# Slot numbers carried in the node's row, one-hot columns made ahead, and the adjacency matrix loaded in two parts

## The chip, the cores and the metric

One core of a Trainium2 chip runs the whole kernel. The time is the device time in microseconds (us) of one execution. The names of the engines are those of the profile: PE is TensorE (PEld its weight loads), DVE is VectorE, ACT is ScalarE, POOL is GpSimd, SP is SyncE. P = 128 is the number of partitions, N = 2048 the nodes, so there are NT = 16 tiles of 128 nodes, and 16 tiles of 128 rows of the adjacency matrix (1 MB each).

## The reference, cut to what matters

Four graph layers follow one another, each with a residual and a layer norm. Only the first one is touched. Its work on 8 graphs with 2048 nodes, 64 features and 64 hyperedges is:

```python
h = x @ W                                             # per node
alpha = softmax(where(H.T > 0, leaky_relu(h @ a_node), NEG))   # per hyperedge, over nodes
agg = einsum('ben,bnf->bef', alpha, h)                # 64 hyperedges: a small table
beta = sigmoid((h @ a_gn)[:, None, :] + (agg @ a_ge)[:, :, None])
all_he = elu(beta * h + (1 - beta) * agg)             # per pair (hyperedge, node)
se = tanh(elu(agg) @ fcW + fcb) @ av
coefs1 = softmax(where(H > 0, se, NEG))               # per node, over its hyperedges
g = einsum('bne,benf->bnf', coefs1, all_he)           # the loop that the change is about
deg = maximum(adj.sum(-1), 1.0)
industry = einsum('nm,bmf->bnf', adj / deg, x @ W_ind)  # the large product, beside it
# ... attention over (industry, g), residual, layer norm; then layers 1 to 3
```

Few pairs (hyperedge, node) are set in H. The kernel sorts the nodes by how many hyperedges they have (`order`), and handles a tile of 128 sorted nodes slot by slot: slot s is the s-th hyperedge of each node. A one-hot matrix (hyperedge by node) picks the right row of the table with a matrix product.

## The kernel before

First phase: for each tile of nodes a projection `ph`, exponentials, a sum over nodes `pagg` for the table, and a row of 520 values (features and gates) written to HBM. The adjacency streams in meanwhile and is cast.

```python
def load_adj(t):
    for k in range(2):
        a = pa.tile([P, HN], F32, tag="a", name="a", bufs=4)
        nc.sync.dma_start(a, adj_t[t * P:(t + 1) * P, cols(k, HN)])
        if t < NT - XT:  nc.gpsimd.tensor_copy(adj[t][:, cols(k, HN)], a)     # tiles 0 to 11
        else:            nc.scalar.copy(adj[t][:, cols(k, HN)], a)            # tiles 12 to 15
# ... cut ...
hs = pa.tile([P, NT, E], F32, name="hs")         # the mask's rows in sorted order
for t in range(NT):
    nc.gpsimd.indirect_dma_start(out=hs[:, t, :], in_=h_ne, in_offset=... order[:, t:t + 1] ...)
# ... cut ...
for t in range(NT):                              # the first phase's loop
    # 4 products into ph, exponentials, products with them (DVE), then:
    nc.scalar.dma_start(hs_hbm[t * P:(t + 1) * P, :], st)      # row: 512 features, 8 gates
    for k in range(2):
        nc.tensor.matmul(pagg[:, k, ...], lhsT=m_n[:, t, :], rhs=ex[:, k] ...)
xs_scope.close()                                 # frees the room of adjacency tiles 12 to 15
for t in range(NT - XT, NT): load_adj(t)
degrees(0, 8)                                    # 4 products per tile: column sums of adj
# slot numbers: compares, 16 transposes, 4 products with a triangle of ones, into `slot`
# table of the hyperedges and se, with degrees(8, 10), (10, 12), (12, 16) between; ts2
```

The row gathers follow, and a loop over 16 tiles of sorted nodes. PE is filled up in it with the products `u` of the industry term, x split into a high and a low half (`v0h`, `v0l`, ...) against the resident adjacency.

```python
def split(pool, src, tag, bufs, shape):
    nc.scalar.copy(hi, src)
    nc.vector.tensor_tensor(lo, src, hi, ALU.subtract)         # low half on DVE

def begin(t):
    hrow = pl.tile([P, BF + 8], F32, tag="hrow", name="hrow", bufs=2)
    nc.gpsimd.indirect_dma_start(out=hrow, in_=hs_hbm[:], in_offset=... order[:, t:t + 1] ...)
    both = split(pb, hrow[:, 0:BF], "hr", 2, [P, BF])
    for s in range(S):                                         # S slots in this tile
        nc.gpsimd.tensor_scalar(o, slot[:, cols(t, P)], float(s + 1), None, op0=ALU.is_equal)
        mm(ps[:, s] ..., lhsT=o, rhs=ts2)
    # R, rs, co: small operations of DVE

now = begin(0)
for t in range(NT):
    for s in range(S):
        mm(pz, ...)                          # 3 products: row high, row low, table by one-hot
        if s == 0 and t + 1 < NT:
            fill(3); now = begin(t + 1)
        fill(8)                              # 8 products u
        nc.vector.tensor_tensor(z, z, R ...)           # DVE, in PSUM
        nc.scalar.activation(y, z, AF.Exp, bias=-1.0)  # ACT
        nc.vector.scalar_tensor_tensor(y, z, 1.0, y, op0=ALU.max, op1=ALU.min)
        # s == 0: acc = y * co on DVE; else y = y * co on DVE, acc += y on POOL
```

Of the kernel before, what the change touches and what calls it, by code (L numbers as in the profile page):

```python
# [56 lines left out]
def tile_gnn_fast(  # L57
# [6 lines left out]
    h_ne: bass.AP,  # L64
# [24 lines left out]
    E = h_ne.shape[1]  # L89
# [72 lines left out]
    def split(pool, src, tag, bufs, shape):  # L162

        hi = pool.tile(shape, F32R, tag=f"{tag}h", name=f"{tag}h", bufs=bufs)
        lo = pool.tile(shape, F32R, tag=f"{tag}l", name=f"{tag}l", bufs=bufs)
        nc.scalar.copy(hi, src)  # L166
        nc.vector.tensor_tensor(lo, src, hi, ALU.subtract)
        return hi, lo
# [33 lines left out]
    slot = hy.tile([P, N], BF16, name="slot")  # L202

    inv_row = hy.tile([P, N], F32, name="inv_row")
    tri2 = hy.tile([P, P], BF16, name="tri2")
    nc.vector.memset(tri2, 0.0)
    make_upper_triangular(nc, tri2[0:E, 0:E], 1.0, diag=True)
    nc.vector.tensor_copy(tri2[E:P, E:P], tri2[0:E, 0:E])

    hs_hbm = dram.tile([N, BF + 8], F32, name="hs_hbm")  # L210
# [7 lines left out]
    XT = NT // 4  # L218
    adj = [adj_pool.tile([P, N], F32R, name=f"adj{t}") for t in range(NT - XT)]




    with tc.tile_pool(name="pa", bufs=1) as pa, tc.tile_pool(name="pa_ps", bufs=1, space=PSUM) as pps:
# [3 lines left out]
        nc.sync.dma_start(m_n, h_ne.rearrange("(t p) e -> p t e", p=P))  # L228
# [15 lines left out]
        def load_adj(t):  # L244

            HN = N // 2
            for k in range(2):
                a = pa.tile([P, HN], F32, tag="a", name="a", bufs=4)
                nc.sync.dma_start(a, adj_t[t * P:(t + 1) * P, cols(k, HN)])
                if t < NT - XT:  # L250
                    nc.gpsimd.tensor_copy(adj[t][:, cols(k, HN)], a)
                else:
                    nc.scalar.copy(adj[t][:, cols(k, HN)], a)

        for t in range(NT - XT):
            load_adj(t)
# [59 lines left out]

        tl = pa.tile([P, NT], F32, name="tl")
# [29 lines left out]

        hs = pa.tile([P, NT, E], F32, name="hs")
        for t in range(NT):
            nc.gpsimd.indirect_dma_start(  # L350
                out=hs[:, t, :], out_offset=None, in_=h_ne,
                in_offset=bass.IndirectOffsetOnAxis(ap=order[:, t:t + 1], axis=0),
            )

# [19 lines left out]
        for t in range(NT):  # L374
            ph = pps.tile([P, 2, C], F32, tag="ph", name="ph", bufs=2)
            for p in range(NP):
                nc.tensor.matmul(
                    ph[:, p // 2, (p % 2) * 2 * (F + 2):(p % 2 + 1) * 2 * (F + 2)], lhsT=xt[t][:, p, :],
                    rhs=bd66.rearrange("p b f -> p (b f)"), start=True, stop=True,
                )  # L380
            hv = ph[:, :, 0:G * (F + 2)].rearrange("p k (g c) -> p k g c", c=F + 2)
            st = pa.tile([P, BF + 8], F32, tag="st", name="st", bufs=2)
            ex = pa.tile([P, 2, G, F + 1], F32, tag="ex", name="ex", bufs=2)
            sv = seen[:, t].rearrange("p (k g) c -> p k g c", k=2)
            nc.vector.tensor_scalar(
                sv, hv[:, :, :, F:F + 2], CLIP, -CLIP, op0=ALU.min, op1=ALU.max
            )
            e_gn = st[:, BF:BF + 8]
            nc.scalar.activation(e_gn.rearrange("p (k g) -> p k g", k=2), sv[:, :, :, 1], AF.Exp)
            lr = pa.tile([P, B], F32, tag="lr", name="lr", bufs=2)  # L390
            nc.vector.scalar_tensor_tensor(
                lr, seen[:, t, :, 0], 0.2, seen[:, t, :, 0], op0=ALU.mult, op1=ALU.max
            )
            nc.scalar.activation(ex[:, :, :, F], lr.rearrange("p (k g) -> p k g", k=2), AF.Exp)
            for k in range(2):
                nc.vector.scalar_tensor_tensor(
                    st[:, k * G * F:(k + 1) * G * F].rearrange("p (g f) -> p g f", f=F), hv[:, k, :, 0:F], 1.0,
                    e_gn[:, k * G:(k + 1) * G, None].to_broadcast([P, G, F]), op0=ALU.add, op1=ALU.mult,
                )
            nc.vector.tensor_tensor(  # L400
                ex[:, :, :, 0:F], hv[:, :, :, 0:F], ex[:, :, :, F:F + 1].to_broadcast([P, 2, G, F]), ALU.mult
            )
            nc.scalar.dma_start(hs_hbm[t * P:(t + 1) * P, :], st)
            for k in range(2):
                nc.tensor.matmul(
                    pagg[:, k, 0:G * (F + 1)], lhsT=m_n[:, t, :], rhs=ex[:, k].rearrange("p g c -> p (g c)"),
                    start=t == 0, stop=t == NT - 1,
                )
# [6 lines left out]
        for t in range(NT - XT, NT):  # L415
            adj.append(adj_end.tile([P, N], F32R, name=f"adj{t}"))
            load_adj(t)


        du = [pps.tile([P, 2, C], F32, tag="ph", name=f"du{g}", bufs=2) for g in range(2)]  # L420
        ones_r = pa.tile([P, P], F32R, name="ones_r")
        nc.gpsimd.tensor_copy(ones_r, ones)

        def degrees(first, end):
            for t in range(first, end):
                for c in range(NCH):
                    mm(
                        du[c // 2][:, c % 2, :], lhsT=ones_r, rhs=adj[t][:, cols(c)],
                        start=t == 0, stop=t == NT - 1,
                    )  # L430

        degrees(0, 8)


        for c in range(NCH):
            m2 = pa.tile([P, JT, 2, E], F32, tag="m2", name="m2", bufs=2)
            for i in range(2):
                nc.vector.tensor_scalar(m2[:, :, i, :], hs[:, c * JT:(c + 1) * JT, :], 0.0, None, op0=ALU.is_gt)
            pt = pps.tile([P, C], F32, tag="sm", name="pt", bufs=2)
            for j in range(JT):  # L440
                nc.tensor.transpose(pt[:, cols(j, P)], m2[:, j].rearrange("p i e -> p (i e)"), ident)
            mt = pa.tile([P, C], BF16, tag="mt", name="mt", bufs=2)
            nc.scalar.copy(mt, pt)
            pcm = pps.tile([P, C], F32, tag="sm", name="pcm", bufs=2)
            nc.tensor.matmul(pcm, lhsT=tri2, rhs=mt, start=True, stop=True)
            nc.vector.tensor_tensor(slot[:, cols(c)], pcm, mt, ALU.mult)
# [12 lines left out]
        tab = pa.tile([E, B, F], F32, tag="st", name="tab", bufs=2)  # L459
# [21 lines left out]
        degrees(8, 10)  # L481
# [7 lines left out]
        degrees(10, NT - XT)  # L489
# [4 lines left out]
        degrees(NT - XT, NT)  # L494
# [9 lines left out]
        for g in range(2):  # L504
            nc.scalar.copy(inv_row[:, cols(g, 2 * C)], du[g].rearrange("p k c -> p (k c)"))
# [34 lines left out]
    with ExitStack() as pb_scope:  # L540
        pb = pb_scope.enter_context(tc.tile_pool(name="pb", bufs=1, side="right"))
        pps = pb_scope.enter_context(tc.tile_pool(name="pb_ps", bufs=1, space=PSUM))
        def products():
# [3 lines left out]
            def fetch(p, c):  # L547
                xc[p, c] = pb.tile([P, JT, P], F32, tag="x", name="xc", bufs=4)
                load_x(xc[p, c], p, c)
# [3 lines left out]
            def parts(p, c):  # L553
                part[c] = split(pb, xc.pop((p, c)), f"v{c}", 1, [P, JT, P])

            for c in range(NCH):
                fetch(0, c)
            for c in range(NCH):
                parts(0, c)
            deg1 = pb.tile([P, NT], F32, name="deg1")  # L560
            for p in range(NP):
                for g in range(2):
                    own = (2 * g, 2 * g + 1)
                    u = {c: pps.tile([P, C], F32, tag=f"u{c}", name=f"u{c}", bufs=1) for c in own}
# [36 lines left out]

        filler = products()
# [6 lines left out]

        def begin(t):  # L610

            hrow = pl.tile([P, BF + 8], F32, tag="hrow", name="hrow", bufs=2)
            nc.gpsimd.indirect_dma_start(
                out=hrow, out_offset=None, in_=hs_hbm[:],
                in_offset=bass.IndirectOffsetOnAxis(ap=order[:, t:t + 1], axis=0),
            )
            S = sum(n > t for n in SLOT_TILES)
            both = split(pb, hrow[:, 0:BF], "hr", 2, [P, BF])
            ohs = []
            ps = pps.tile([P, 12, 2, B], F32, tag="ps", name="ps", bufs=1)  # L620
            for s in range(S):
                o = pl.tile([P, P], F32R, tag="o", name="o", bufs=17)
                nc.gpsimd.tensor_scalar(o, slot[:, cols(t, P)], float(s + 1), None, op0=ALU.is_equal)
                ohs.append(o)
# [15 lines left out]

        now = begin(0)
        for t in range(NT):
            S, both, ohs, R, co = now
            acc = pl.tile([P, B, F], F32, tag="acc", name="acc", bufs=2)
            for s in range(S):
# [6 lines left out]
                fill(8)  # L652
# [15 lines left out]

    hy_scope.close()
# [459 lines left out]
def tile_gnn_general(  # L1129
# [643 lines left out]
    "x", "x_t", "adj_t", "h_ne", "w0", "w_ind", "a_node", "a_gn", "a_ge", "fc_w", "fc_b", "av", "w1_t",  # L1773
    "emb", "emb_t", "w_pool", "b_pool", "iv", "w31_t", "b31", "w32_t", "w32", "b32", "w0_t",
# [66 lines left out]
```

## Time and profile before

| | before |
|---|---|
| median of 4 runs beside the changed kernel | 2229.9 us (2225.27 to 2233.65) |
| last product of the first phase (`pagg` ends) | 78.9 us |
| G: first row gather | 101.3 us |
| first product with a low half of x | 114.2 us |
| end of the loop (last product u) | 293.1 us |
| from there to the end | 1934.1 us |

### The profile page before, as it was taken

The page shows a single profiled execution, that of the slowest core. Times are in us where ns is not written, and L with a number is a line of the kernel's source. Part 1 is how long each engine was busy: PE and PEld are TensorE (multiplying, and loading weights), DVE is VectorE, ACT ScalarE, POOL GpSimd, SP SyncE. Part 2 cuts the span into 40 slices and gives each one's busy share as a digit, 9 for nine tenths or more (in the row PEclk, how much of TensorE's full clock was granted, in tenths as well). Part 3 has the DMA queues.
Part 4 walks back from the last instruction along what each step waited for, and adds up shares of the span by engine and source line. Part 5 has one row for each costly group of instructions (what it writes and reads, how often), then busy time and mean ns, then how long its engine had stood idle before and what let it go on. Part 6 is the DMA issues. An engine that isn't in the chain of part 4 may idle for free.

```text
span 2227.2 us, 19810 instructions
## 1 busy us (share of the span) xinstructions
PE 1993.1 (89%) x7318; PEld 1289.3 (58%) x7318; DVE 1139.1 (51%) x1900; ACT 338.3 (15%) x584; POOL 551.0 (25%) x499
## 2 busy tenths in 40 slices
PE   7799978888759999799999999999986989999994
PEld 4488745555644444375456456447434777777873
DVE  5479956666532222216864773782784344331312
ACT  1322323222111111010010001001000011111110
POOL 5457466564323323200110110110010001010202
PEclk7889989999969999999999999999998999999997
DMA  8723334322210000000000000000001223200000
GB/s 263 237 66 91 95 91 107 83 70 63 76 46 0 19 19 19 19 24 5 10 5 3 10 8 1 10 8 3 8 8 32 76 72 85 62 19 1 20 1 21
DMA packets 99306, 103.26 MB, mean 46 GB/s; under 512 B 63088, under 2 KB 63136, under 8 KB 99008
## 3 DMA queue, kind: packets, MB, share of 16 engines
q1 hardware_dynamic: 73248, 83.09, 12.8%
q0 software_dynamic: 4064, 9.10, 1.7%
q10 hardware_dynamic: 21888, 9.70, 1.6%
q8 instruction: 60, 0.98, 0.2%
q14 instruction: 46, 0.38, 0.1%
HBM read 75.59 MB, written 26.28 MB: 46 GB/s over the span
## 4 chain that ended last, share of the span: by engine, by line
PE 63%; DVE 12%; DMA 12%; POOL 7%; issue 4%; ACT 2%; SPq 0%; ACTq 0%; POOLq 0%; DVEq 0%
PE py L967 18%; PE u L171 17%; PE u L914 10%; PE u L527 9%; DMA fcav<-in_adj_t 7%; POOL ln_r L155 3%; PE pz L171 2%; DVE fcav L1061 2%; PE pf L171 1%; PE pr L171 1%; DMA x<-x_hbm 1%; DVE ln_v L151 1%; DVE ln_c L145 1%; DVE ln_m L143 1%; ACT r L149 1%
## 5 line engine op out<-in xcount | busy, mean ns | idle before, releaser
L967 PE MATMUL py<-wp,xg 128*128 128x512 f32 x1024 | 448.5, 597 | 8.5 <-DVE fcav L972 5.8
L967 PEld LDWEIGHTS py<-wp,xg 128*128 128x128 f32 x1024 | 193.6, 191 | 254.4 <-issue 216.4
L171 PE MATMUL u<-adj,hi 128*128 128x512 f32 x768 | 256.5, 415 | 0.0
L171 PE MATMUL u<-adj,lo 128*128 128x512 f32 x768 | 246.5, 400 | 1.1 <-DVE lo L1026 1.1
L914 PE MATMUL u<-pt,xn 128*128 128x512 f32 x512 | 227.5, 603 | 8.3 <-DVE u L923 7.1
L972 DVE TENSOR_TENSOR fcav<-py,emb_n 128x512 f32<-128x512 f32 x256 | 177.0, 691 | 52.0 <-PE py L967 37.5
L975 POOL TENSOR_TENSOR r<-r,bias 128x256 f32<-128x256 f32 x32 | 23.3, 729 | 636.0 <-DVE r L973 636.0
L973 DVE TENSOR_REDUCE r<-fcav 128x32 f32<-128x512 f32 x256 | 175.4, 685 | 8.1
L914 PEld LDWEIGHTS u<-pt,xn 128*128 128x128 f32 x512 | 97.3, 193 | 130.2 <-issue 114.7
L527 PE MATMUL u<-adj,vh 128*128 128x512 f32 x512 | 158.3, 408 | 15.4 <-ACT vh L166 11.6
L171 PEld LDWEIGHTS u<-adj,hi 128*128 128x128 f32 x768 | 143.2, 190 | 40.8 <-issue 11.5
L171 PEld LDWEIGHTS u<-adj,lo 128*128 128x128 f32 x768 | 144.6, 190 | 35.4 <-DVE lo L1026 1.6
L527 PE MATMUL u<-adj,vl 128*128 128x512 f32 x512 | 152.1, 398 | 0.0
L155 POOL TENSOR_TENSOR ln_r<-ln_e,neg_half 128x8 f32<-128x8 f32 x64 | 106.1, 1658 | 174.9 <-DVE ln_e L153 166.9
L908 DVE TENSOR_SCALAR pt<-pt 128x512 f32<-128x512 f32 x64 | 49.1, 784 | 172.8 <-ACT pt L907 171.3
L1045 POOL TENSOR_TENSOR r<-r,xn 128x512 f32<-128x512 f32 x16 | 20.4, 1275 | 418.9 <-DVE r L1044 418.9
L527 PEld LDWEIGHTS u<-adj,vh 128*128 128x128 f32 x512 | 96.2, 189 | 45.7 <-ACT vh L166 13.1
L912 POOL TENSOR_TENSOR acc<-acc,pt 128x512 f32<-128x512 f32 x60 | 79.6, 1327 | 162.6 <-DVE pt L908 159.8
L527 PEld LDWEIGHTS u<-adj,vl 128*128 128x128 f32 x512 | 96.4, 189 | 22.1 <-issue 0.7
L1061 DVE SCALAR_TENSOR_TENSOR fcav<-fcav,adj 128x512 f32<-128x512 f32 x64 | 44.5, 695 | 117.6 <-DMA fcav<-in_adj_t 117.1
L149 ACT ACTIVATE r<-ln_c 128x512 f32<-128x512 f32 x64 | 40.4, 631 | 288.4 <-DVE ln_c L145 274.8
L709 POOL DMA_INDIRECT gn<-gs_hbm,rank x64 | 69.7, 1088 | 34.7 <-issue 14.2
(316 smaller groups left out, 2774.3 us busy)
## 6 DMA issues: line engine op xcount, KB each, us to landing
a<-in_adj_t SPq DMA_DIRECT2D x32, 512.0 KB, 5.9
fcav<-in_adj_t SPq DMA_DIRECT2D x64, 256.0 KB, 2.8
x_hbm<-r SPq DMA_DIRECT2D x20, 256.0 KB, 2.3
hs_hbm<-st ACTq DMA_DIRECT2D x16, 260.0 KB, 5.4
xt<-in_x_t SPq DMA_DIRECT2D x16, 256.0 KB, 5.4
u_hbm<-ut SPq DMA_DIRECT2D x16, 256.0 KB, 2.7
gs_hbm<-acc SPq DMA_DIRECT2D x16, 256.0 KB, 2.0
ut<-u_hbm SPq DMA_DIRECT2D x16, 256.0 KB, 3.2
```

Source lines behind the costliest of these rows:

```text
L149: nc.scalar.activation(r, xc, AF.Square)
L155: nc.gpsimd.tensor_tensor(rstd, vare, neg_half[:, :groups], ALU.pow)
L171: tc.keep_in_program_order(nc.tensor.matmul(*args, **kw))
L527: nc.tensor.matmul(u[c], lhsT=half[:, j, :], rhs=adj[t][:, cols(c)], start=t == 0 and i == 0, stop=ends and not own,)
L709: nc.gpsimd.indirect_dma_start(out=gn[:, j, :], out_offset=None, in_=g_rows, in_offset=bass.IndirectOffsetOnAxis(ap=rank4[:, p, c * JT + j ...
L908: nc.vector.tensor_scalar(pt, pt, 1.0, None, op0=ALU.max)
L912: nc.gpsimd.tensor_tensor(acc, acc, pt, ALU.add)
L914: nc.tensor.matmul(u[p], lhsT=xn[p][:, t, :], rhs=pt, start=t == 0, stop=t == NT - 1)
L967: nc.tensor.matmul(py.rearrange("p o d -> p (o d)"), lhsT=xg[b][:, q, cols(j, P)], rhs=wp[:, q, cols(k)], start=q == 0, stop=q == 1,)
L972: nc.vector.tensor_tensor(pr, py, e_b, ALU.mult)
L973: nc.vector.tensor_reduce(r[:, j, b, cols(k, OH)], pr, AX.X, ALU.add)
L1061: nc.vector.scalar_tensor_tensor(a, a, 1.0, adj[t][:, cols(k)].bitcast(F32), op0=ALU.mult, op1=ALU.not_equal, accum_out=left[:, t, k:k + 1],)
```

## The change

Its intent, as far as it can be read from the code: take the slot numbers out of POOL's sixteen mask gathers (they are computed at the front in node order and travel in the row that is gathered anyway), prepare the one-hot columns before their tile begins, and let the first row gather start without waiting for the whole adjacency. Nine tiles are loaded before it and seven after. The degrees, which need all tiles, become the first filler products of the loop. Side changes come with it, above all four: row buffers 2 to 4, load buffers 4 to 3, the low halves of x on POOL, and all casts of the adjacency on POOL.

```diff
-    def split(pool, src, tag, bufs, shape):
+    def split(pool, src, tag, bufs, shape, eng=nc.vector):
-        nc.vector.tensor_tensor(lo, src, hi, ALU.subtract)
+        eng.tensor_tensor(lo, src, hi.bitcast(F32) if eng is nc.gpsimd else hi, ALU.subtract)
+    HROW = BF + 8 + E
+    EARLY = 9
-                a = pa.tile([P, HN], F32, tag="a", name="a", bufs=4)
+                a = pa.tile([P, HN], F32, tag="a", name="a", bufs=3)
-        for t in range(NT - XT):
+        for t in range(EARLY):
             load_adj(t)
+        mt = pa.tile([E, N], BF16, name="mt")
+        nc.vector.tensor_scalar(mt, m_en, 0.0, None, op0=ALU.is_gt)
+        for t in range(NT):
+            nc.tensor.matmul(pcm[:, t, :], lhsT=mt[:, cols(t, P)], rhs=tri_e, start=True, stop=True)
+        nc.vector.tensor_tensor(slot, pcm, m_n, ALU.mult)
-        hs = pa.tile([P, NT, E], F32, name="hs")            # and 16 gathers of the mask
-            st = pa.tile([P, BF + 8], F32, tag="st", name="st", bufs=2)
+            st = pa.tile([P, HROW], F32, tag="st", name="st", bufs=4)
+            nc.scalar.copy(st[:, BF + 8:], slot[:, t, :])
-        for t in range(NT - XT, NT):
-            load_adj(t)
-        degrees(0, 8)                                       # and the old slot numbers
+        some_degrees(5)                                     # later 2 and 2; 28 products stay
@@ the loop @@
-                part[c] = split(pb, xc.pop((p, c)), f"v{c}", 1, [P, JT, P])
+                part[c] = split(pb, xc.pop((p, c)), f"v{c}", 1, [P, JT, P], nc.gpsimd)
+            yield from degree_passes
+        def load_adj_end(t):
+            for c in range(NCH):
+                a = pb.tile([P, JT, P], F32, tag="x", name="a", bufs=XB)...   # shared with x
+                nc.sync.dma_start(a, adj_t[t * P:(t + 1) * P, cols(c)])
+                tc.keep_in_program_order(nc.gpsimd.tensor_copy(adj[t][:, cols(c)], a))
+        def slots(t):
+            transpose(pt, hrows[t][:, BF + 8:])
+            for i in range(2):
+                nc.scalar.copy(slot[i * E:(i + 1) * E, :], pt)
+            # then one is_equal per slot on POOL, kept in one_hot[t]
+        fetch_rows(0)
+        fetch_rows(1)
+        for t in range(EARLY, EARLY + 2):
+            load_adj_end(t)
+        slots(0)
+        for t in range(EARLY + 2, NT):
+            load_adj_end(t)
         now = begin(0)
+        slots(1)
-                fill(8)
+                fill(4 if t == 0 and s < 6 else 8)
+                if s == max(0, S - 5) and t + 2 < NT:
+                    slots(t + 2)
```

## The prediction

> **What bounds the kernel now.** I read first the page's table of 40 slices and its chain by line. TensorE (PE) is busy 89% of 2227 us, and all the lines that cost much (L967, L914, L527, the products with the adjacency after 293 us) belong to later layers. The order in which each engine issues after the loop over 16 tiles of nodes is the same in both builds (ACT, POOL and SP word for word), so I carry that part, 293 us to the end, over unchanged. All that can move lies in 0 to 293 us. There I took the busy time by stage:
>
> ```profile
> core 0: us, PE busy (x) PEld busy (x) DVE busy (x) ACT busy (x) POOL busy (x), PEclk, DMA share, GB/s
> 16.00:60.00 44.00, 35.19 (x157) 22.59 (x157) 26.18 (x80) 4.42 (x20) 27.05 (x27) 0.73 0.82 265
> 60.00:79.00 19.00, 14.22 (x56) 8.25 (x57) 14.08 (x33) 3.24 (x12) 11.35 (x12) 0.73 0.92 321
> 79.00:101.00 22.00, 19.00 (x88) 13.29 (x87) 6.04 (x14) 12.16 (x18) 2.22 (x2) 1.00 0.65 207
> 101.00:113.00 12.00, 6.62 (x16) 4.82 (x17) 2.45 (x8) 2.89 (x5) 10.58 (x18) 0.50 0.55 133
> 113.00:135.00 22.00, 21.47 (x82) 17.46 (x81) 10.60 (x24) 2.83 (x5) 9.11 (x10) 0.66 0.33 72
> 135.00:239.00 104.00, 104.00 (x477) 85.72 (x476) 99.32 (x180) 34.37 (x59) 74.56 (x74) 1.00 0.28 82
> 239.00:264.00 25.00, 21.45 (x95) 16.84 (x93) 24.96 (x47) 7.47 (x13) 10.27 (x9) 1.00 0.26 85
> ```
>
> The reader sees three regimes: DMA near its limit until 79 us, a seam from 79 to 113 us in which nothing is full except POOL at the end, and then a loop in which PE is full, with VectorE (DVE) hardly less so, and DVE alone full at 239 to 264 us. The chain that ended last names what holds the first two:
>
> ```profile
> 52.26 5.42 DMA hs<-in_h_ne,order
> ...
> 64.77 7.27 DMA hs_hbm<-st
> ...
> 94.40 4.22 DMA a<-in_adj_t
> 98.62 0.02 issue
> 98.65 1.04 ACT adj L253
> 99.69 0.92 ACT inv_row L505
> 100.61 0.70 issue
> 101.31 6.49 DMA hrow<-hs_hbm,order
> ```
>
> The first gather of rows (hrow, 101.31) waits for the last adjacency tile, its cast on ACT and the evacuated degrees. Before that, the gathers of the mask (hs) stand in POOL's queue and hold both DVE and the loads. The waits of 0 to 101 us, those of the load queue and of ACT, say it again:
>
> ```profile
> SPq L249 <- POOL adj L251: 39.6, 21, 7.8
> ACT st L389 <- DVE seen L385: 38.0, 11, 9.4
> ACT st L389 <- DMA hs_hbm<-st: 16.7, 5, 6.0
> ```
>
> **What the Trainium skill says.** "DMA: Bandwidth & Descriptors", Specifications, puts HBM for one core at about 358 GB/s. The trace agrees roughly: stretches of 4 us in which the DMA is over 92% busy show 282 to 389 GB/s, a little over the page at the top. "TensorE: Matmul & The Clock Gate", Part 1, says that PE runs at half clock after an idle window and needs some 3.4 us of work to come back. The trace agrees: granted clock 0.50 at 101 to 113 us, where PE waits for one-hots, and 0.66 in the next stage. "GPSIMD Engine Reference", 3.1, says that a two-input elementwise operation is nearly twice as slow on GpSimd as on VectorE. The trace agrees: acc (128x512) takes 1294 ns on POOL in the middle, a like product on DVE 680 ns. "SBUF — State Buffer", Who interferes with whom, says that such operations of both engines lock each other out. The loop's acc mean of 1381 ns over that median fits, though it doesn't prove it.
>
> **The change, part by part.**
>
> (1) Slot numbers move to the front. Gone are 16 mask gathers on POOL (15.4 us busy, 23 us with their waits), 8 DVE compares, 16 PE transposes and 4 products. New at about 11 to 14 us are a DVE compare of 64x2048 (twice the 0.76 us of the 128x1024 one, 1.5 us), 16 small bf16 products (some 1.3 us) and one DVE product of 128x1024 (1.2 us). In the build these stand ahead of the first ph products, so the first pagg goes from 16.3 to about 20 us: 3 to 4 us lost. Gained is the pause at 40 to 44 and 57 to 62 us, where PE waited 2.95 us and 4.72 us for DVE behind the mask gathers.
>
> (2) Row writes with four buffers. A tile costs PE 1.06 us for ph and 1.06 us for pagg: 2.15 us at full clock, as at 32 to 40 us. But in ACT's order of the changed build the slot copy for tile k+2 stands before the second exp of tile k and waits for the write of tile k-2. So four buffers help little more than two, and with a write landing in 5.4 us (median) the beat is about (5.4+0.8)/2 = 3.1 us while loads fill the DMA. Adjacency loads before the seam shrink from 16.8 to 9.4 MB, so they end at some 52 us; the beat falls to 2.15 us from there. Tiles 0 to 3 done at 35.5 us, then 12 tiles at 2.4 us on the mean: pagg ends near 64.5 us instead of 78.9.
>
> (3) The seam. From pagg's end to ts2 it is 14.7 us now (78.9 to 93.6). With 20 instead of 32 degree products ahead of pht it becomes about 12.5 us. The gather then waits for nothing of the later adjacency: it goes at G = 64.5 + 12.5 = 77 us instead of 101.3. That is 24 us gained at this point.
>
> (4) The price: tile 0. Seven adjacency tiles (7.3 MB, 22 us at 330 GB/s) now load after G, 28 casts of 128x512 on POOL. In POOL's order of the changed build, between the first gather and the first low half v0l, stand: 4 gathers x 1.15 = 4.6 us; 17 one-hots x 0.555 = 9.4; 28 casts x 0.57 (between half of the 1.05 us cast of 1024 and the 609 ns least copy of 512) = 16.0; 5 acc x 1.29 = 6.5; v0l 1.3. Sum 37.8 us, and some 3 us until the first row and slots are there: 41 us. PE reaches the first product with v0l (pz of 8 slots and 28 degree products done) only then, at 77 + 41 = 118 us. Before, it had this at 114 us. So part 4 eats all of the 24 us and more; only the work done in the meantime remains as gain.
>
> (5) The rest of the loop, PE's bill from the chain: 8 products u take 1.83 us (0.229 each), a pz triple 0.70, ps 0.115. After v0l: 512 x 0.229 = 117.2; 49 pz x 0.70 = 34.3; 40 ps x 0.115 = 4.6; pdc about 3 (now 4.57 at half clock); pinv 1.8; 14 new slot transposes x 0.11 = 1.5. Sum 162.4 us. The loop now: 117.2 + 56 x 0.70 + 45 x 0.115 + 4.57 + 1.8 = 168 us of 180 us from 112.8 to 292.9, so 12 us are lost to half clock at the start and to DVE at 239 to 264 us. The 16 low halves v (x 0.68 = 11 us) leave DVE for POOL, which has room (POOL was 72% busy at 135 to 239 us). I put the loss at 7 us: 169.4 us. End of loop 118 + 169 = 287 us against 293: about 6 us gained.
>
> **The rivals.** (A) POOL blocks less than I count, or the ph loop runs at PE's beat throughout: G near 72, tile 0 in 37 us; end at 278 us, time 2214. For it: the parameters look tuned. Against: the order in POOL's queue. (B) The first phase stays bound by DMA. 19.5 MB have to pass before G (x 4.2, adjacency 9.4, rows 4.8, masks 1.0); at the 265 GB/s of 16 to 60 us that is 73 us, and pagg ends at 70 us or later, the writes still on the path: loop end at 293 us or more, time 2230. For it: three load buffers instead of four. Against: the 265 GB/s was measured with POOL holding the loads. (C) POOL becomes the bound in the steady loop: low halves waiting for PE and ACT hold acc, y has two buffers, DVE and PE stop behind it. 16 halves with 1 us each would make 2238. For it: POOL executes in order. Against: a quarter of its time was free. (D) All 24 us are kept, if tile 0 hides behind PE's own work: 2203. Against: PE has only some 13 us of work there.
>
> **Range and chances.** My sum gives 2229.6 - 6 = 2223 us. Each us of G and of tile 0 counts fully; I am unsure by 5 us on each, by 4 on the loop's losses, so about 8 us in all: 2207 to 2236. Two per cent is 44.6 us; the whole seam and tile 0 are worth less, so faster by over 2% has a chance of 0.02, slower by over 2% 0.01, the rest 0.97.
>
> **What would show it.** Right: the first row gather at 72 to 82 us; pagg ending 12 to 13 us before; from there 38 to 45 us in which POOL is over 85% busy, PE not; the first v0l product near 118 us, waiting for POOL; DVE busy less by some 10 us in the loop, and the stage before its end with less PE idle time; the end of the loop near 287 us; the time from there to the end within 2 us of before. Wrong: a first gather after 85 us (the ph loop is still held by the row writes), PE at work through tile 0 (POOL cheaper than counted), or new waits of PE for the low halves or of ACT for acc in the steady loop.

## More of the kernel before

From the page of the kernel before, busy time and share of the span by engine:

```profile
span 2227.2 us, 19810 instructions
PE 1993.1 (89%) x7318; PEld 1289.3 (58%) x7318; DVE 1139.1 (51%) x1900; ACT 338.3 (15%) x584; POOL 551.0 (25%) x499
```

The shares are averages over four layers. Only the first 293 us can change, and there they differ from stage to stage. So the milestones above are what to compare; each is the start or end of one instruction in the timeline. A sum over them tells where a difference was made: first phase up to G, the first tile (G to the first low-half product), the loop proper, the rest.

## The result, and the profile after

The changed kernel took 2247.38 us in the median of 4 runs (2244.34 to 2249.93) against 2229.9 us. The ratio is 1.0079 with a 95% interval of 1.0054 to 1.0104. Its output is correct. Ratios here and below are the mean time of one kernel's fast runs over the mean of the other's in the same rounds, so not quite the ratio of the medians quoted.

Within 2% it is "the same", yet it is slower by more than the runs scatter, and lies outside the predicted range. Set against the milestones of before:

| us | before | predicted | after |
|---|---|---|---|
| `pagg` ends | 78.9 | 64.5 | 73.7 |
| G: first row gather | 101.3 | 77 | 86.6 |
| first product with a low half | 114.2 | 118 | 135.8 |
| end of the loop | 293.1 | 287 | 311.7 |
| from there to the end | 1934.1 | 1934 | 1936.4 |

The loss is made in the loop's stretch alone. Loop end: -14.7 us up to G, +36.3 us in the first tile (12.9 before, 49.2 now), -3.0 us in what follows (178.9 before, 175.9 now). That makes +18.6 us; the rest adds 2.3 us, which is within what it varies between runs of one instruction order (1925 to 1941 us over the runs below).

Busy time by stage of the changed kernel, with columns as in the prediction's first fence:

```profile
core 0: us, PE busy (x) PEld busy (x) DVE busy (x) ACT busy (x) POOL busy (x), PEclk, DMA share, GB/s
16.00:60.00 44.00, 32.05 (x163) 20.96 (x162) 27.65 (x92) 6.59 (x35) 16.64 (x16) 0.84 0.88 299
60.00:74.00 14.00, 11.94 (x66) 7.80 (x66) 9.64 (x30) 2.38 (x13) 2.08 (x2) 1.00 0.49 172
74.00:86.60 12.60, 10.76 (x60) 8.35 (x58) 5.18 (x13) 3.16 (x8) 0.03 (x1) 0.96 0.00 1
86.60:110.00 23.40, 10.86 (x29) 8.02 (x30) 5.81 (x16) 2.77 (x7) 17.25 (x29) 0.50 0.52 162
110.00:135.00 25.00, 17.11 (x42) 10.35 (x41) 11.49 (x17) 5.65 (x9) 20.24 (x27) 0.70 0.79 223
135.00:190.00 55.00, 53.85 (x248) 43.51 (x248) 36.80 (x62) 17.30 (x34) 36.87 (x35) 0.92 0.26 70
```

Two things are to be seen. From 74 to 86.6 us the DMA engines stand still (1 GB/s): the late loads take over memory of the first phase and wait for its last operation (their queue waits 11.4 us for the table `ts`). And in the 48 us after G, the stage of the first tile, no engine is full: PE works 28 us at clocks of 0.50 and 0.70, POOL 37.5 us, and the DMA, now carrying 7.3 MB that used to arrive earlier, is busy half to four fifths of the time. Before, this stretch had 12.9 us.

The waits of the changed kernel, engine and line, what was waited for, us in total, times, and the longest; from 0 to 87 us:

```profile
POOL hrow L621 <- DVE ts L499: 21.2, 1, 21.2
ACT st L393 <- DMA hs_hbm<-st: 14.0, 4, 5.2
```

and from 86 to 136 us:

```profile
PEld du L172 <- POOL adj L606: 10.2, 10, 2.6
ACT y L692 <- POOL adj L606: 5.7, 1, 5.7
POOL o L638 <- ACT slot L634: 4.0, 2, 3.3
ACT y L692 <- DMA xc<-in_x: 3.9, 1, 3.9
POOL adj L606 <- DMA a<-in_adj_t: 3.2, 5, 1.3
```

The gather now waits only for the table (`ts`), as intended. But ACT's copy of the slot numbers waits for row writes, and in the first tile everybody waits for everybody: PE's degree products for casts, casts for loads, the one-hots for ACT's slot numbers (which wait for a gathered row that shares the DMA with the loads). Even ACT's exponentials come late: the 5.7 us in the fence end at 125.09 us, just after DVE's product at 125.00, and the PE product before it stands in PE's order behind degree products that wait for casts. The 3.9 us are a wait behind the start of a load of x (129.13 us), which ACT issues too.

The chain that ended last, from 40 to 60 us in the changed kernel (start, us, what), shows the first of these at its worst:

```profile
45.79 8.16 DMA hs_hbm<-st
...
53.98 0.02 ACT st L393
...
54.13 0.22 ACT ex L400
```

A row write of 8.16 us holds ACT's slot copy (L393), and the exponential that PE needs (L400) stands behind it in ACT's order.

### The profile page after: what moved, and what is told of

The parts are those of the page before. It is cut to its first block, busy times and chain, and to the rows that moved or that the text cites. A ratio compares the mean times of both kernels' runs of the same rounds, so it can differ in the third digit from the quotient of the medians.

```text
span 2248.1 us, 19875 instructions
## 1 busy us (share of the span) xinstructions
PE 1997.3 (89%) x7330; PEld 1288.0 (57%) x7330; DVE 1130.2 (50%) x1872; ACT 338.1 (15%) x620; POOL 560.5 (25%) x521
## 4 chain that ended last, share of the span: by engine, by line
PE 58%; DVE 13%; DMA 10%; POOL 9%; issue 5%; ACT 2%; SPq 1%; ACTq 0%; POOLq 0%; DVEq 0%
PE py L1004 18%; PE u L172 12%; PE u L951 10%; PE u L521 9%; DMA fcav<-in_adj_t 7%; POOL ln_r L156 3%; PE ug L172 2%; DVE fcav L1098 2%; POOL gn L746 1%; PE pr L172 1%; DVE ln_c L146 1%; DVE ln_v L152 1%; DVE ln_m L144 1%; ACT r L150 1%; PE pf L172 1%
## 5 line engine op out<-in xcount | busy, mean ns | idle before, releaser
L521 PEld LDWEIGHTS u<-adj,vh 128*128 128x128 f32 x512 | 96.4, 190 | 45.3 <-ACT vh L167 12.6
L746 POOL DMA_INDIRECT gn<-gs_hbm,rank x64 | 69.8, 1091 | 47.9 <-PE pg L175 16.0
```

The lines of the kernel that those rows point to most:

```text
L521: nc.tensor.matmul(u[c], lhsT=half[:, j, :], rhs=adj[t][:, cols(c)], start=t == 0 and i == 0, stop=ends and not own,)
L746: nc.gpsimd.indirect_dma_start(out=gn[:, j, :], out_offset=None, in_=g_rows, in_offset=bass.IndirectOffsetOnAxis(ap=rank4[:, p, c * JT + j ...
```

## The experiments

Thirteen kernels were run. Milestones of their profiled runs (G to low = first row gather to the first product with a low half; loop = from there to the loop's end):

| run | pagg ends | G | G to low | loop | loop's end | time, ratio to before |
|---|---|---|---|---|---|---|
| before | 78.9 | 101.3 | 12.9 | 178.9 | 293.1 | |
| changed | 73.7 | 86.6 | 49.2 | 175.9 | 311.7 | 1.0079 |
| e1 no late loads | 76.6 | 98.9 | 19.6 | 186.0 | 304.5 | 1.0043 |
| e2 12 tiles early | 72.1 | 85.0 | 40.5 | 177.6 | 303.1 | 1.0057 |
| e3 half the casts on ACT | 73.4 | 86.3 | 45.1 | 174.3 | 305.7 | 1.0054 |
| e4 slots by one DMA | 65.1 | 78.0 | 48.3 | 175.3 | 301.6 | 1.0053 |
| e5 = e1 + low halves on DVE | 75.4 | 97.2 | 16.8 | 174.7 | 288.7 | 0.9988 |
| e6 before + low halves on POOL | 78.5 | 101.2 | 15.5 | 181.1 | 297.8 | 1.0056 |
| e7 before + slot transposes | 78.2 | 102.4 | 12.9 | 179.6 | 294.9 | 1.0013 |
| e8 = e2 + e3 + e4 + low on DVE | 65.9 | 78.8 | 34.3 | 179.7 | 292.8 | 0.9996 |
| e9 changed + low on DVE | 71.6 | 84.5 | 48.3 | 175.2 | 308.0 | 1.0081 |
| e10 = e5 + e4 | 64.3 | 95.2 | 16.9 | 176.1 | 288.2 | 0.9956 |
| e11 = e10 + 4 load buffers | 65.8 | 88.5 | 16.9 | 176.9 | 282.3 | 0.9951 |
| e12 changed, no late transfers | 71.0 | 83.9 | 45.7 | 174.0 | 303.6 | slow path |
| e13 changed, a quarter of the bytes | 74.7 | 87.6 | 43.5 | 174.7 | 305.8 | slow path |

All but e12 and e13 are correct by the fast path. Three groups of runs shared the runs of the kernel before (2227.05, 2229.33 and 2227.94 us in the median). Differences of a fraction of a per cent in the time are no more certain than their intervals; the milestones of a single profiled run are exact for that run, but the time from the loop's end on scatters by some 16 us over the table, and `pagg` ends anywhere from 71.0 to 74.7 us in the five runs that share the code before it (changed, e3, e9, e12, e13). So 2 to 4 us between two milestones can be scatter.

### e1: the split undone

```diff
-    EARLY = 9
+    EARLY = NT - XT                    # 12; tiles 12 to 15 again loaded after xs_scope.close()
-                tc.keep_in_program_order(nc.gpsimd.tensor_copy(...))    # all casts on POOL
+                # tiles 12 to 15 cast by ACT, as before; no load_adj_end; degrees 8, 2, 2, 4
-                fill(4 if t == 0 and s < 6 else 8)
+                fill(8)
```

> The changed kernel with the split of the adjacency undone: all 16 tiles loaded, cast and summed into degrees before the first row gather, eight fillers in every slot, the rest as changed (slot numbers in the row, one-hots ahead, four row buffers, low halves on POOL). Theory 1 (tile 0 after the seam is bound by POOL and the loads: 28 casts, 17 one-hots, the adds and the low halves in one queue, 49 us in which PE has 13 us of work, against 12.5 us before): the time from first gather to first product with a low half falls from 49 us to below 22 us, the first gather comes at 92 to 100 us, the end of the loop at 280 to 292 us, time 2217 to 2230. Theory 2 (the loss comes from the low halves on POOL and the slot transposes in the steady loop): the loop after the first low half stays as slow, and the time stays above 2240.

Measured: 2238.03 us, ratio 1.0043 (1.0004 to 1.0082). The first tile shrinks from 49.2 to 19.6 us, but G is back at 98.9, and the loop's end, expected at 280 to 292 us, came at 304.5. So the split costs, by the loop's end, 7.2 us of the 18.6, and something else costs more: the loop proper takes 186.0 us, 7 more than before. This is the second theory for this run (low halves on POOL, slot transposes); both hold in part, and the time lies between what the two had named. e5 to e7 tell its two halves apart.

### e2, e3, e4: three ways to shorten the first stretch

e2 loads 12 tiles before the gathers:

```diff
-    EARLY = 9
+    EARLY = 12
```

> The changed kernel with 12 instead of 9 tiles loaded before the first gather, 16 casts after it instead of 28. The DMA is nearly idle from 66 to 86 us in the changed kernel, so three tiles more (3.1 MB, about 9 us) should fit in front of a gather that waits for pagg. Theory 1: first gather at 86 to 89 us, first low half 8 to 11 us sooner after it (12 casts x 0.63 = 7.6 us, and their loads), time 2236 to 2241. Theory 2: no change, 2245 to 2250.

Measured: 2239.43 us, ratio 1.0057 (1.0018 to 1.0097). G hardly moved (85.0), so three more tiles fit before the gather for nothing; the first tile fell from 49.2 to 40.5 us. Each tile moved ahead saves about 3 us (8.7 / 3). The loop's end moved by 8.6 us.

e3 lets ACT do every second late cast:

```diff
-                tc.keep_in_program_order(nc.gpsimd.tensor_copy(adj[t][:, cols(c)], a))
+                if c % 2: nc.scalar.copy(adj[t][:, cols(c)], a)
+                else:     tc.keep_in_program_order(nc.gpsimd.tensor_copy(adj[t][:, cols(c)], a))
```

> The changed kernel with every second of the 28 casts after the first gather on ACT instead of POOL. If POOL's queue alone sets tile 0, 14 x 0.63 = 9 us go: time 2236 to 2240. If the loads set it (7.3 MB at 330 GB/s are 22 us, and five buffers of 256 KB), at most 4 us go; if ACT's casts hold up ACT's exponentials, nothing or a loss.

Measured: 2238.76 us, ratio 1.0054 (1.0015 to 1.0094). POOL's casts in the first tile fell from 17.5 to 9.8 us; the first tile got only 4.1 us shorter. POOL's waits for loads grew instead, from 3.2 to 7.7 us. So POOL's queue alone does not make the 49 us.

e4 sends the slot numbers into the rows by one DMA of their own, so that ACT has no copies to make:

```diff
+        nc.scalar.dma_start(hs_hbm[:, BF + 8:].rearrange("(t p) e -> p t e", p=P), slot)
-            st = pa.tile([P, HROW], F32, tag="st", name="st", bufs=4)
-            nc.scalar.copy(st[:, BF + 8:], slot[:, t, :])
+            st = pa.tile([P, BF + 8], F32, tag="st", name="st", bufs=4)
```

> The changed kernel with the slot numbers written to DRAM by one transfer of their own instead of by an ACT copy into every row tile: the copy, which waits for the write of the row two tiles back, no longer stands before the second exp. Theory: the stall at 49 to 54 us goes, pagg ends at 65 to 69 us instead of 73.7, the first gather comes 4 to 8 us sooner, and the time falls by as much, to 2239 to 2244. Rival (the row write is slow because loads fill the DMA, whoever waits): pagg ends no sooner.

Measured: 2238.16 us, ratio 1.0053 (1.0011 to 1.0095). `pagg` ends at 65.1 instead of 73.7 us, G comes at 78.0 instead of 86.6, the loop's end 10.1 us earlier. What ACT waited for longest from 0 to 78 us in this run:

```profile
ACT st L395 <- DVE seen L391: 33.4, 15, 12.9
ACT L395 <- DVE fcav L372: 18.9, 1, 18.9
```

The wait for row writes (14.0 us before) is gone, with the same four buffers and the same bytes. This shows that ACT's copy, which waits for row writes, held the first phase, and not a DMA that is full. `pagg` then ends within 1 us of the 64.5 predicted; but the prediction had reckoned that number with the copies in place, so this is in part luck.

### e5, e6, e7: what made the loop longer

Theory A: the low halves on POOL, two-input operations, lock DVE out of memory. Theory B: the transposes of the slot numbers take `pz`'s PSUM buffers and ACT's time.

e5 is e1 with one word less:

```diff
-                part[c] = split(pb, xc.pop((p, c)), f"v{c}", 1, [P, JT, P], nc.gpsimd)
+                part[c] = split(pb, xc.pop((p, c)), f"v{c}", 1, [P, JT, P])
```

> The kernel without the split (first run of this series), with the 16 low halves of x back on DVE as in the kernel before. That kernel took 186.0 us from its first low-half product to the end of the loop, the kernel before 178.9. Theory A (the low halves on POOL cost the loop: two-input work on POOL keeps DVE off the shared SBUF ports and the halves no longer fill gaps in DVE's order): 186 falls to 177 to 181 us, end of the loop at 295 to 299 us. Theory B (the slot transposes sharing the three pz buffers cost it): stays at 184 to 188 us.

Measured: 2224.98 us, ratio 0.9988 (0.9964 to 1.0011). The loop takes 174.7 instead of 186.0 us, its end is 15.8 us earlier: more than the 177 to 181 us that theory A had named.

e6 goes the other way: the kernel before with the low halves on POOL and nothing else (the same `eng` argument as in the change).

> The kernel before with one part of the change alone: the 16 low halves of x on POOL. Theory A: the 178.9 us from the first low-half product to the end of the loop grow by 4 to 8 us. Theory B: no growth, or a gain of up to 4 us, since DVE gives away 11 us of work.

Measured: 2242.05 us, ratio 1.0056 (1.0037 to 1.0075). The loop's end is 4.7 us later. The loop itself grew by only 2.2 us, less than the 4 to 8 expected; 2.6 us are the first tile's. Of the 9.8 us that the spans differ, 5 came after the loop, where nothing was changed; so the ratio says that it is slower, and its size is uncertain.

e7 adds to the kernel before 14 transposes of a dummy in `pz`'s buffers, each with two ACT copies, at the places that the change uses:

```diff
+        def slots():
+            pt = pps.tile([E, P], F32, tag="mm", name="pslot", bufs=3)
+            transpose(pt, bd_ind[:, 0:E])
+            for i in range(2):
+                nc.scalar.copy(slot2[i * E:(i + 1) * E, :], pt)
+                if s == max(0, S - 5) and t + 2 < NT:
+                    slots()
```

> The kernel before with another part alone: in 14 of the 16 tiles a 64-row transpose into one of the three buffers of pz, and two copies of it on ACT into a tile that nobody reads (the right result stays). Theory B: the 178.9 us grow by 4 to 8 us. Theory A: by at most 2 us, the PE time of the transposes themselves.

Measured: 2234.22 us, ratio 1.0013 (0.9984 to 1.0043); the loop 179.6 against 178.9 us. Theory B falls: 0.7 us.

What theory A says of DVE is seen in its groups by line and form, from 135 to 300 us (count, then busy us and mean ns, then idle time before). The same two products, with low halves on POOL, in e1:

```profile
L701 DVE TENSOR_TENSOR y<-y,co 128x512 f32<-128x512 f32 x40 | 34.5, 863 | 0.4
L699 DVE TENSOR_TENSOR acc<-y,co 128x512 f32<-128x512 f32 x14 | 12.9, 919 | 0.0
```

and in e5, with the low halves on DVE:

```profile
L701 DVE TENSOR_TENSOR y<-y,co 128x512 f32<-128x512 f32 x38 | 28.1, 742 | 0.2
L699 DVE TENSOR_TENSOR acc<-y,co 128x512 f32<-128x512 f32 x15 | 10.8, 723 | 0.0
```

In the kernel before, for comparison:

```profile
L663 DVE TENSOR_TENSOR y<-y,co 128x512 f32<-128x512 f32 x39 | 28.9, 747 | 0.1
L661 DVE TENSOR_TENSOR acc<-y,co 128x512 f32<-128x512 f32 x15 | 10.5, 698 | 0.0
```

and in e6, which differs from it by the low halves alone:

```profile
L663 DVE TENSOR_TENSOR y<-y,co 128x512 f32<-128x512 f32 x40 | 35.8, 898 | 0.4
L661 DVE TENSOR_TENSOR acc<-y,co 128x512 f32<-128x512 f32 x15 | 14.1, 939 | 0.0
```

An operation of these two forms takes 121 to 241 ns longer when POOL makes the low halves, in either pair. The two forms that read their product from PSUM do not change (`pz<-pz,R` 685 to 687 ns, `y<-pz,y` 681 to 685 ns in all four runs). Of e1 against e5: 40 x 0.121 + 14 x 0.196 = 7.6 us more for DVE. The 12 halves that fall into this stretch took DVE 10.3 us in e5. So the move relieved DVE of little; its busy time in the loop is 159.3 us in e1 against 160.7 in e5. And it put 1.3 us operations into POOL's queue in front of `acc` and the one-hots.

That explains why nothing was gained, but not the 11.3 us by which e1's loop is longer. DVE, as busy in both, stands idle for 26.7 us in e1 and 14.0 in e5; 13.0 against 4.2 us of this are waits for ACT's exponentials. PE idles 7.2 against 2.3 us, at a mean clock of 0.95 against 0.99. Whether the longer operations or the halves' place in POOL's queue (rival C) make DVE wait is not shown: no run has one without the other. That the move of the low halves costs this is shown.

### e8: all three repairs together, with the split kept

e2, e3 and e4 and the low halves on DVE in one kernel.

> The changed kernel with four mends at once: 12 tiles loaded early, half of the later casts on ACT, the slot numbers written by a transfer of their own, the low halves on DVE. By the single runs the first product with a low half should come at 110 to 116 us (78 + 32 to 38) and, if theory A holds, the end of the loop 168 to 174 us later, at 280 to 288 us: 5 to 13 us less than the kernel before. If theory B holds, it is near 288 to 292 us, level with the kernel before.

Measured: 2229.79 us, ratio 0.9996 (0.9977 to 1.0015), the loop's end at 292.8 instead of the 280 to 288 expected, near the range named for theory B, which e7 rules out. G is at 78.8, and the first tile still takes 34.3 us. Busy time by stage of this run, from its G on:

```profile
core 0: us, PE busy (x) PEld busy (x) DVE busy (x) ACT busy (x) POOL busy (x), PEclk, DMA share, GB/s
78.80:113.10 34.30, 19.83 (x70) 14.19 (x70) 14.50 (x30) 12.62 (x24) 22.05 (x32) 0.75 0.67 193
113.10:140.00 26.90, 22.49 (x89) 18.58 (x89) 16.29 (x24) 5.66 (x11) 14.31 (x12) 0.75 0.19 44
140.00:276.50 136.50, 133.42 (x606) 107.43 (x605) 131.93 (x257) 49.30 (x100) 78.73 (x79) 1.00 0.29 91
276.50:292.80 16.30, 16.27 (x72) 13.00 (x70) 4.66 (x8) 0.60 (x1) 1.29 (x1) 1.00 0.17 64
```

From 140 to 276.5 us PE is busy 98% and DVE 97% of the time, and the last 16 us are almost all products u. So what the first 61 us after G lose in clock (0.75) and idle time is never made up, and with it goes the gain of the earlier gather. The 28 degree products that the split leaves for the loop are not in this full stretch: all of them run before 113.1 us, where PE is busy 19.8 of 34.3 us.

### e9: the changed kernel with the low halves on DVE

The edit of e5, on the changed kernel.

> The changed kernel with the low halves of x back on DVE and nothing else. It closes a table of two by two: end of the loop 304.5 us without the split and 288.7 us without the split and with the halves on DVE, 311.7 us for the changed kernel. If the two costs simply add, this ends at 311.7 - 15.8 = 296 us, and the split costs some 7 us by itself. If the halves cost more where POOL is crowded, it ends sooner than 293; if the split keeps PE waiting whatever DVE does, not before 300.

Measured: 2245.44 us, ratio 1.0081 (1.0055 to 1.0107): no gain in time, 3.7 us at the loop's end (not before 300, the third case). Of these, 2.1 us were there at `pagg`'s end already, where the edit changes nothing; the loop itself takes 175.2 instead of 175.9 us. Together with e1 and e5 this gives a table of four for the loop's end:

| | low halves on POOL | low halves on DVE |
|---|---|---|
| split | 311.7 | 308.0 |
| no split | 304.5 | 288.7 |

The two costs do not add. With the split, low halves on POOL cost 3.7 us at most, which is within the scatter; without it 15.8. The split costs 7.2 us with the low halves on POOL, 19.3 without them. A plausible reason is that PE, delayed by the first tile, leaves DVE time to catch up; no run isolates this.

### e10, e11: the parts that help, alone

e10 is e5 with e4's edit: no split, low halves on DVE, slots in the row by their own DMA. e11 gives the loads their fourth buffer back:

```diff
-                a = pa.tile([P, HN], F32, tag="a", name="a", bufs=3)
+                a = pa.tile([P, HN], F32, tag="a", name="a", bufs=4)
```

> No split, low halves on DVE, and the slot numbers written by a transfer of their own. The stall behind the row writes goes, so pagg should end at 65 to 69 us instead of 75.4, the space for the last four adjacency tiles comes free as much sooner, and the first gather goes at 89 to 93 us instead of 97.2. If the loads are what holds the gather, it goes at 95 us or later. The loop after it should take as long as in the kernel with the halves on DVE: end at 280 to 285 us in the first case, 0.3 to 0.6% faster than the kernel before.

> The same with four load buffers for the adjacency instead of three. If the loads of the first 60 us are held by the buffers, the gather comes up to 3 us sooner still; if the DMA is full, no change within 1 us.

Measured, 5 rounds each: e10 2218.62 us, ratio 0.9956 (0.9936 to 0.9976); e11 2216.53 us, ratio 0.9951 (0.9931 to 0.9971). In e10, `pagg` ends 11 us earlier than in e5, but G only 2 us, at 95.2 and not at the 89 to 93 expected: the gather waits for the whole adjacency again, and the loads, with three buffers, are late. The fourth buffer brings G to 88.5, 6.7 us and not the 3 at most that I had expected. Both kernels beat the one before. Between each other they are not told apart by time.

### e12, e13: casts or bytes in the first tile?

e12 leaves the late transfers out; the casts read a constant. e13 transfers a quarter and lets the cast repeat it. The degrees are wrong, so the kernel's own check sends it on to its slow path, which makes the output right and the time 7621 us. That time says nothing, and only the stretch up to the loop's end is read, from one run each, whose state is unknown.

```diff
 # e12
-                nc.sync.dma_start(a, adj_t[t * P:(t + 1) * P, cols(c)])
-                ... nc.gpsimd.tensor_copy(adj[t][:, cols(c)], a)
+                ... nc.gpsimd.tensor_copy(adj[t][:, cols(c)], ones repeated)
 # e13
+                nc.sync.dma_start(a[:, 0:P], adj_t[t * P:(t + 1) * P, c * C:c * C + P])
+                ... nc.gpsimd.tensor_copy(adj[t][:, cols(c)], a[:, 0:P] repeated)
```

> The changed kernel without the transfers of its seven late adjacency tiles (7.3 MB); the 28 casts that follow stay on GpSimd, at their places, but read a constant of ones, so the degrees and the output are wrong on purpose. What makes up the 49.2 us between the first row gather and the first product with a low half is asked for. If GpSimd's queue holds it (28 casts of 647 ns, one-hot columns, low halves of 1.3 us, one behind the other), it stays at 45 us or more. If the transfers hold the queue (the casts wait for them, the x loads stand behind them on the DMA engines), it falls to some 36 us: 28 casts of 0.65 us, four halves of 1.3 us and the one-hot columns of the first slots are left, and casts no longer wait. The first row gather should stay at 84 to 89 us (the load's memory waits end only after it), and the loop's end move by what the stretch gives, less what its own products take: 12 to 0 us earlier than 311.7.

> The changed kernel with the same 28 late transfers and casts, but each transfer brings 64 KB instead of 256 KB and the cast repeats it four times, so the degrees are wrong on purpose and the checked slow path follows; only the stretch before it is read. Unlike the run without transfers, the one-hot columns of the second tile stand between the casts again, as in the changed kernel. In that run GpSimd reached v0l 31.8 us after the first row gather instead of 47.9, but its order had moved, and PE came only 3.5 us sooner. If the bytes make GpSimd's queue late, v0l is reached 32 to 37 us after the gather on GpSimd and PE has its first product with it at 35 to 40 us instead of 49.2. If the casts and the slots' own round over the engines make it, both stay within 4 us of the changed kernel: 44 us or more.

Measured in e12: the first tile takes 45.7 us, which is what "POOL's queue" had asked for. But the timeline does not bear its reason out: POOL began `v0l` 31.8 us after the gather (115.72 against 83.90), in the changed kernel 47.9 us after (134.48 against 86.57). The casts, no longer waiting, had moved ahead of the second tile's one-hots in POOL's order, and PE waited for those. So e12 told nothing apart, and e13 keeps the one-hots between the casts.

Measured in e13: POOL begins `v0l` 37.2 us after the gather (124.77 against 87.61), just at the end of the 32 to 37 expected if the bytes hold it. PE has its first low-half product after 43.5 us, between the two expectations (35 to 40, or 44 and more). But POOL's order had moved here too: two adds `acc` stand before `v0l` instead of five. Of the 10.7 us by which `v0l` begins sooner, 4.0 are work that now comes after it (POOL is busy 33.0 us before it instead of 37.0), and 6.7 are idle time that is gone (4.2 instead of 10.9 us). So the bytes make POOL late by some 7 us, not by all of the 10.7.

Of the 10.7 us, PE got 5.7. The timeline of ACT in e13 (start, us, line, operation) shows where the rest went:

```profile
124.85 0.60 ACT L694 ACTIVATE y<-pz 128x512 f32<-128x512 f32 x1 [2.66 <-POOL acc L702]
128.50 0.60 ACT L694 ACTIVATE y<-pz 128x512 f32<-128x512 f32 x1 [2.03 <-POOL acc L702]
129.00 1.92 ACT L558 COPY inv_row<-du 128x1024 f32<-128x1024 f32 x2
```

PE, done with the degrees at 123.3 us, needs their buffers for its first product u, and so waits for ACT's copy of them (`inv_row`):

```profile
130.05 1.22 PE L172 MATMUL ug<-adj,v0h 128*128 128x512 f32 x2 [6.78 <-ACT inv_row L558]
```

The copy stands in ACT's order behind two exponentials that wait for adds of POOL, and the second of these adds stands in POOL's order behind `v0l` (124.77) and `v1l`:

```profile
126.00 1.26 POOL L168 TENSOR_TENSOR v1l<-xc,v1h 128x512 fp32r<-128x512 f32 x1
127.22 1.25 POOL L702 TENSOR_TENSOR acc<-acc,y 128x512 f32<-128x512 f32 x1
128.44 1.25 POOL L168 TENSOR_TENSOR v2l<-xc,v2h 128x512 fp32r<-128x512 f32 x1
129.66 1.26 POOL L168 TENSOR_TENSOR v3l<-xc,v3h 128x512 fp32r<-128x512 f32 x1
```

This is close to what rival C had named for the loop: low halves hold the adds, and ACT, DVE and PE stop behind them. Beside it, one product of DVE that takes 0.69 us elsewhere in the same timeline (122.00, for one) lasts 4.78 us:

```profile
126.69 4.78 DVE L701 TENSOR_TENSOR y<-y,co 128x512 f32<-128x512 f32 x1
```

It ends at 131.47 us, just after the last of four back-to-back two-input operations of POOL (130.92). PE had gone on by then (130.05), so this is not what held it.

So the 49.2 us have two layers. The bytes account for some 7 us of POOL's lateness. Under them lies a second limit of about 44 us, made of casts, one-hots, adds and low halves in one queue and of the waits of ACT behind it: e12, without any of these bytes, still takes 45.7 us. What each of them is worth in it is not shown.

## Why the prediction was wrong

The terms of its sum, each against its measurement, add up to the miss of the loop's end:

| term | predicted | measured | miss |
|---|---|---|---|
| G | 77 | 86.6 | +9.6 |
| first tile | 41 | 49.2 | +8.2 |
| loop proper | 169.4 | 175.9 | +6.5 |
| loop's end | 287 | 311.7 | +24 |

**Part 2, the beat of the first phase: the step that failed first.** The prediction saw that ACT's slot copy for tile k+2 stands ahead of the second exponential of tile k and waits for a row write. It then reckoned with a write of 5.4 us until 52 us and PE's own beat after that. The first four tiles were done at 36.3 us, against 35.5 in the sum; the miss came after them. The writes were not that regular: one of 8.16 us stopped ACT, and `pagg` ended at 73.7 and not 64.5 us. e4 shows the cause: it takes the copies out of ACT's order and gets 65.1. The prediction had named this sign of being wrong itself: a first gather after 85 us. Rival B had the right symptom (writes still on the path, `pagg` at 70 us or later), but its reason, that the DMA bounds the phase, is not what e4 shows: with the same bytes it went away.

**Part 3, the seam: right.** 12.9 us from `pagg`'s end to the gather against 12.5 predicted, and the gather waits for the table alone. What the prediction missed is that the loads stand still for those 12.6 us.

**Part 4, the price of tile 0: mechanism right, size off.** It foresaw that the seven late tiles and POOL's queue eat more than the gain of the earlier gather. The busy part was sized well: the prediction added 37.8 us of POOL's work, and POOL is busy 38.3 of the 49.2 us. The mis-sized term is POOL's idle time: the sum had "some 3 us until the first row and slots are there", and POOL idles 10.9 us. The waits for slots took 4.0 of these, nearly as predicted; what the sum left out are the waits for loads (3.2 us), for DVE (1.7) and smaller ones. In e13, with a quarter of the bytes, 6.7 of the 10.9 us are gone. The prediction had also said POOL would be over 85% busy here; it was 78%.

**Part 5, the loop: the side step failed in sign.** "The 16 low halves v leave DVE for POOL, which has room" was counted as a gain. POOL had time, but two forms of DVE's operations took 121 to 241 ns longer beside the moved work. The prediction quoted the lock between the two engines, saw a sign of it in the mean of `acc`, and then did not apply it to the work it moved. e5 against e1 shows 11.3 us of loop and 15.8 us at its end; e6 shows the same direction on the kernel before, with 2.2 us of loop; inside the changed kernel itself, e9, it is worth 0.7 us of loop and nothing measurable in time. So it does not explain the changed kernel's miss of 6.5 us in the loop. The mis-sized term there is the loss beside PE's bill of 162.4 us, put at 7 us and measured at 13.5: PE is busy 7.8 us beyond the bill, at a mean clock of 0.98, and idles 5.7 us. What makes these stays open. One reading behind the term was wrong: the prediction took the 0.66 of 113 to 135 us for agreement with the 3.4 us of work that it quotes. In the kernel before PE works without a gap from 114.8 us, and its granted clock is still 0.50 from 119 to 121 us. And most of the 4.57 us of `pdc`, billed as at half clock, ran at 0.92 to 0.94.

**Rival C** (POOL the bound of the loop, 16 halves with 1 us each, 2238 us) was closest in the time and in the direction, and wrong in the place: most of the loss lay in the first tile. There e13 shows a mechanism close to its own; in the loop it is not told apart from the operations' cost to DVE. (Rival D's 2203 us is 2 us below its own sum, 2229.6 less 24.) **The carried part**, 293 us to the end, held within 2.3 us. The range was too narrow: the three misses (9.6, 8.2 and 6.5 us) were each larger than the 5, 5 and 4 us allowed for them, and all went the same way.

In sum: the gather came 14.7 us earlier, and the first tile took 36.3 us more, of which undoing the split takes 29.6 back (e1); there PE ran at clocks of 0.50 and 0.70, and the loop had no slack to make it up. What is left of the change without the split, the low halves on POOL and ACT's copies (slot numbers without mask gathers, one-hots made ahead, four row buffers, not told apart) is worth 0.4 to 0.5% (e10, e11).

## What to carry to other kernels

Work taken from in front of a wait has to be paid somewhere: before moving a load behind the first use, look whether the stage it goes to has slack on the engine that ends it, or only looks idle because it waits. An engine's free time is not by itself room for more work: ask what the moved operations cost the neighbour they relieve, and what they stand in front of. When a small copy is put in an in-order queue, ask what stands behind it: here 16 copies of 0.24 us, waiting for row writes, held the first phase for 8.6 us, and one DMA of its own did the same without.

## What the Trainium skill lacked or had wrong

- "SBUF — State Buffer", Who interferes with whom, says that the second of two contending operations blocks until the first finishes. It does not say what happens when the winner's queue goes on: in e13 a DVE product of 0.69 us lasted 4.78 us, until after the last of four POOL operations in a row. This is one instance.
- "GPSIMD Engine Reference", 3.1, gives 769 ns for 512 elements as measured in the best case, a tight loop, and no figure for the whole fixed cost of a small operation. Here POOL's cast of 128x512 took 647 ns on the mean, so less than that, and the one-hot compare of 128x128, a quarter of the elements but another operation, still 567 ns on the mean.
- "TensorE: Matmul & The Clock Gate", Part 1, ties the half clock to idle time of PE. It does not say that PE can lose its clock while the profile shows it busy: in the kernel before, PE has no gap from 121 to 131 us, and the granted clock falls from 0.94 (123 to 125 us) to 0.50 (125 to 131 us) at the end of 32 products of one element each (`pdc`, 122.2 to 126.8 us). In the changed kernel it falls after `pdc` too (0.78 at 146 to 148 us, 0.50 at 148 to 150).
